# One pass of exponentials and gate for all tokens, and half of the columns turned by DMA

## The chip, the core and the metric

The kernel runs on one core of a Trainium2 chip. The core has a matrix engine (TensorE, PE in the profile; its weight loads are listed as PEld), a vector engine (VectorE, DVE), an engine for activation functions (ScalarE, ACT), a general one (GpSimd, POOL) and one that issues transfers (SyncE, SP). Each engine works through its own list of instructions in order, and engines wait for each other on semaphores. The transfers of all queues run on 16 DMA engines.

The metric is the time of the kernel on the device in microseconds (us); smaller is better. A changed kernel is compared with the kernel before on the same chip.

## The reference

All arithmetic is in float32. Eight sequences of 512 tokens with 512 features go through one block:

```python
xn = layernorm(x)                                   # x: (8, 512, 512)
# linear attention, 16 heads of 32
q, k, v = rotate(silu(xn @ Wq)), rotate(silu(xn @ Wk)), xn @ Wv
for chunk in chunks_of_128:                         # with per-head decay
    o = (q @ k.T * D) @ v + (q * decay_q) @ S
    S = lam_C * S + (k * decay_k).T @ v
s = group_rmsnorm(o * sigmoid(xn @ Wg1 @ Wg2)) * norm_weight @ Wo
# 16 experts, 4 of them per token, and a shared one
p = softmax(xn @ gate_w.T); w, e = top_k(p, 4); w = w / w.sum()
mixed = sum(w[r] * swiglu(xn, expert[e[r]]) for r in range(4))
shared = swiglu(xn, shared_expert) * sigmoid(xn @ shared_gate_w)
out = x + s * silu(mixed + shared)
```

Softmax over the 16 followed by the division through the sum of the four is the same as exponentials of the four logits less the largest one, divided by their sum. The kernel computes that.

## The kernel before, in words

A tile is 128 tokens; a sequence has four, and there are 32 in all. The work has these stages:

1. **To about 200 us: routing and shared expert of all eight sequences, beside the attention of sequence 0.** `norm` brings a sequence to mean 0 and variance 1 in place. `turn` transposes it on TensorE (four transposes of 128x128 per tile into one bank of PSUM, `psT`) and ScalarE copies the bank to `xT`, the transposed sequence. `route_1` multiplies it with the router weights (`plT`, 17 columns: 16 experts and the shared gate), `route_2` turns the result back (`pl`, copied to `lg`), `route_3` picks the four largest and makes their weights `w4` and one-hot masks. `share_1` and `share_2` compute the shared expert (`pg`, `pu`, `h`, `pys`), and its rows go to memory (`sh_d`). `halves` splits the upper 256 columns of each row into their 16-bit halves (`hs`) and writes them to `xn_d`, from where the expert blocks gather them.
2. **To about 240 us: `sort`** makes the places of all tokens in the lists of the experts, and sums the weights into rows that lie beside the tokens in `xn_d`.
3. **To about 310 us: attention of sequence 1**, with the tables of the lists made in between.
4. **To about 725 us: expert blocks** of 128 list entries: a gather, transposes (half by TensorE, half by a DMA on the 16-bit halves, joined by ScalarE in `join`), two matrix products and the weighted rows to `y_d`.
5. **To the end: attention of sequences 2 to 7**, beside `mixture`, which gathers four rows of `y_d` per token, adds them to the shared expert's row `m`, and applies Silu.

The order on TensorE in stage 1 is written out by hand: each group is issued `on_pe`, behind the last one. `first` is a generator of the pieces of routing and shared expert, and `along` takes the next one or two pieces between the pieces of the attention. On the other engines a scheduler orders the instructions at build time. It uses eight completion semaphores for the transfers of SyncE in turn, so that each transfer is issued only once the eighth before it is complete.

PSUM has eight banks: four of kind `a` and two of kind `d` that are taken in turn, one `m` and one `k`. A bank is free once its reader is done. ScalarE holds the table of one function at a time; the profile shows each change of it as ACT_TABLE_LOAD. Copies need none.

Lines that the prediction touches: 281 (transposes), 283 (copy of `psT`), 298 (`plT`), 314 (sigmoid of the gate), 331 (exponential), 357 and 637 (Silu of the shared expert, of keys and queries), 372 (shared rows times gate), 583 and 587 (values and their copy), 691 (scores `ps`), 738 and 742 (attention output `po` and its product with `on`), 706, 1076 and 1091 (the nearest rows for new operations), 1220 (mixture).

Of the kernel before, what the change touches and what calls it, by code (L numbers as in the profile page):

```python
# [10 lines left out]
F32 = mybir.dt.float32  # L11
# [3 lines left out]
U16 = mybir.dt.uint16  # L15
AF = mybir.ActivationFunctionType
ALU = mybir.AluOpType
AX = mybir.AxisListType

P = 128  # L20
B, N, D = 8, 512, 512
# [3 lines left out]
NC = N // C  # L25
NT = B * NC
KC = D // P
E, F, TOPK = 16, 128, 4
EA = E + 1
RK = HD  # L30
Q = 32
# [64 lines left out]
def tile_block(ctx: ExitStack, tc: tile.TileContext, a: dict, out: bass.AP):  # L96
    nc = tc.nc
# [3 lines left out]
    dram = ctx.enter_context(tc.tile_pool(name="dram", bufs=1, space=bass.MemoryType.DRAM))  # L101
# [3 lines left out]
    def bank(tag, name):  # L105
        return pp.tile([P, 512], F32, tag=tag, name=name, bufs={"a": 4, "k": 1, "m": 1, "d": 2}[tag])
# [6 lines left out]
    s_d = [dram.tile([N, D], F32, name=f"s_d{b}", tag=f"s_d{b}") for b in range(FIRST)]  # L113
    y_d = dram.tile([NB * P, D], F32, name="y_d", tag="y_d")
    at_d = dram.tile([P, TOPK * NT], I32, name="at_d", tag="at_d")

    def load(pool, name, shape, dt=F32):
        t = pool.tile(shape, dt, tag=name, name=name, bufs=1)
        flat = t if len(shape) == 2 else t.rearrange(
            "p a b -> p (a b)" if len(shape) == 3 else "p a b c -> p (a b c)")  # L120
        nc.sync.dma_start(flat, a[name])
        return t
# [17 lines left out]
    scr1 = left.enter_context(tc.tile_pool(name="scr1", bufs=1, side="left"))  # L140
    p1 = right.enter_context(tc.tile_pool(name="p1", bufs=1, side="right"))

    xs_of = {}

    def load_x(b):
        t = p1.tile([P, NC, D], F32, tag="x", name=f"x_{b}", bufs=3)
# [6 lines left out]
    ident = load(const, "ident", [P, P])  # L153
# [31 lines left out]
    wo = load_w(const, "wo")  # L185

    w4 = p1.tile([P, NT, TOPK], F32, tag="w4", name="w4")
    posi = p1.tile([P, TOPK, NT], I32, tag="posi", name="posi")

    sp = const.tile([P, 2, TOPK * NT], F16, tag="slot", name="sp")  # L190
# [27 lines left out]
        mybir.EngineType.Pool, mybir.EngineType.DVE, mybir.EngineType.Activation)  # L218


    xT_of, xT1_of, plT_of, lg_of, h1_of, sg_of = ({} for _ in range(6))
    oh = p1.tile([P, TOPK, E, NT], F32, tag="oh", name="oh")
    mask = p1.tile([P, E, NT], F32, tag="mask", name="mask")

# [33 lines left out]
    def halves(b):  # L258
        xs = xs_of[b]
        for t in range(NC):  # L260
            hs = p1.tile([P, D], U16, tag="hs", name=f"hs_{b}_{t}", bufs=4)
            with behind(POOL):
                nc.gpsimd.tensor_copy(
                    hs.rearrange("p (h d) -> p h d", h=2),
                    xs[:, t, D // 2 :].bitcast(U16).rearrange("p (d h) -> p h d", h=2))
            g = b * NC + t
            nc.sync.dma_start(xn_d[g * P : (g + 1) * P, D : 2 * D], hs)

    def turn(b):

        xs = xs_of[b]
        if b:
            xT = p1.tile([P, KC, N], F32, tag="xT1", name=f"xT1_{b}", bufs=2)
        else:
            xT = xT_of[b] = att.tile([P, KC, N], F32, tag="xT", name=f"xT_{b}", bufs=1)
        xT1_of[b] = xT
        for t in range(NC):
            ps = bank("a", f"psT_{b}_{t}")
            with on_pe():
                for k in range(KC):  # L280
                    nc.tensor.transpose(
                        ps[:, k * P : (k + 1) * P], xs[:, t, k * P : (k + 1) * P], ident)
            nc.scalar.copy(
                xT[:, :, t * P : (t + 1) * P], ps.rearrange("p (k n) -> p k n", n=P))
        if b:
            xs_of.pop(b)
            if b + 3 < B:
                load_x(b + 3)
            nc.sync.dma_start(xT_d[b], xT.rearrange("p k n -> p (k n)"))
# [16 lines left out]
    def route_2(b):  # L306
        lT = plT_of.pop(b)
        pl = bank("a", f"pl_{b}")
        with on_pe():
            nc.tensor.transpose(pl[:, :P], lT, ident)  # L310
        lg = p1.tile([P, NC, EA], F32, tag="lg", name=f"lg_{b}", bufs=2)
        nc.vector.tensor_copy(lg, pl[:, :P].rearrange("p (t q) -> p t q", q=Q)[:, :, :EA])
        sg = p1.tile([P, NC], F32, tag="sg", name=f"sg_{b}", bufs=2)
        nc.scalar.activation(sg, lg[:, :, E], AF.Sigmoid)
        sg_of[b] = sg
        lg_of[b] = lg

    def route_3(b):
        lg = lg_of.pop(b)
        mx = p1.tile([P, NC, 8], F32, tag="mx", name=f"mx_{b}", bufs=2)  # L320
        ix = p1.tile([P, NC, 8], U32, tag="ix", name=f"ix_{b}", bufs=2)
        for t in range(NC):
            nc.vector.max(mx[:, t, :], lg[:, t, :E])
            nc.vector.max_index(ix[:, t, :], mx[:, t, :], lg[:, t, :E])
        bt = slice(b * NC, (b + 1) * NC)
        nc.vector.tensor_copy(
            idx[:, :, bt].rearrange("p r t -> p t r"), ix[:, :, :TOPK])
        e4 = p1.tile([P, NC, TOPK], F32, tag="e4", name=f"e4_{b}", bufs=2)
        nc.vector.tensor_tensor(
            e4, mx[:, :, :TOPK], mx[:, :, 0:1].to_broadcast([P, NC, TOPK]), ALU.subtract)  # L330
        nc.scalar.activation(e4, e4, AF.Exp)
        den = p1.tile([P, NC], F32, tag="den", name=f"den_{b}", bufs=2)
        nc.vector.tensor_reduce(den, e4, axis=AX.X, op=ALU.add)
        nc.vector.reciprocal(den, den)
        nc.vector.tensor_tensor(
            w4[:, bt, :], e4, den.unsqueeze(2).to_broadcast([P, NC, TOPK]), ALU.mult)

        for q in range(TOPK):
            nc.vector.tensor_tensor(
                oh[:, q, :, bt], idx[:, q, bt].unsqueeze(1).to_broadcast([P, E, NC]),  # L340
                iota_e.unsqueeze(2).to_broadcast([P, E, NC]), ALU.is_equal)
        for q in range(1, TOPK):
            nc.vector.tensor_tensor(
                mask[:, :, bt], mask[:, :, bt] if q > 1 else oh[:, 0, :, bt], oh[:, q, :, bt],
                ALU.add)
# [14 lines left out]
        h1_of[b] = h  # L360

    def share_2(b):
        h, sg = h1_of.pop(b), sg_of.pop(b)
        xT1_of.pop(b)
        for t in range(NC):
            sh = p1.tile([P, D], F32, tag="sh1", name=f"sh1_{b}_{t}", bufs=6)
            py = bank("dama"[t], f"pys_{b}_{t}")
            with on_pe():
                nc.tensor.matmul(
                    py, lhsT=h[:, t * P : (t + 1) * P], rhs=sw[:, KC * 2 * F :],  # L370
                    start=True, stop=True)
            nc.scalar.activation(sh, py, AF.Copy, scale=sg[:, t : t + 1])
            nc.sync.dma_start(sh_d[b][t * P : (t + 1) * P, :], sh)


    def sort():

        wt = p1.tile([P, NT, E], F32, tag="h1", name="wt", bufs=2)
        wr = p1.tile([P, NT, E], F32, tag="sl", name="wr", bufs=2)
        for r in range(TOPK):  # L380
# [12 lines left out]
        for to, by, name in ((total, ones, "total"), (af, tri, "before")):  # L393
            ps = bank("a", f"p{name}")
# [572 lines left out]
    def first():  # L967
# [22 lines left out]
        next(sorting)  # L990

    sorting = sort()
    norm(0)
    turn(0)
    norm(1)
    halves(0)
    xs_of.pop(0)
    load_x(3)
# [174 lines left out]
    with tc.If(count > SURE):  # L1173
# [16 lines left out]
    comb = right.enter_context(  # L1190
        tc.tile_pool(name="comb", bufs=1, side="right", reuse_waits="tile"))

    place = comb.tile([P, TOPK, NT], I32, tag="place", name="place")
    nc.sync.dma_start(place.rearrange("p r t -> p (r t)"), at_d)

    def mixture(b, t):

        g = b * NC + t
        m = comb.tile([P, D], F32, tag="m", name=f"m_{b}_{t}", bufs=12)
        nc.sync.dma_start(m, sh_d[b][t * P : (t + 1) * P, :])  # L1200
        s = None
        if b < FIRST:
            s = comb.tile([P, D], F32, tag="s", name=f"s_{b}_{t}", bufs=4)
            nc.sync.dma_start(s, s_d[b][t * P : (t + 1) * P, :])
        ys = []
        for r in range(TOPK):
            yg = comb.tile([P, D], F32, tag="yg", name=f"yg_{b}_{t}_{r}", bufs=14)
            with behind(POOL):
                nc.gpsimd.indirect_dma_start(  # L1209
                    out=yg, out_offset=None, in_=y_d,  # L1210
                    in_offset=bass.IndirectOffsetOnAxis(ap=place[:, r, g : g + 1], axis=0))
            ys.append(yg)
            yield
        with behind(POOL):
            nc.gpsimd.tensor_tensor(ys[0], ys[0], ys[1], ALU.add)
        yield
        with behind(POOL):
            nc.gpsimd.tensor_tensor(ys[2], ys[2], ys[3], ALU.add)
        with behind(DVE):
            nc.vector.tensor_tensor(m, m, ys[0], ALU.add)  # L1220
        yield
        with behind(DVE):
            nc.vector.tensor_tensor(m, m, ys[2], ALU.add)
        yield
        with behind(ACT):
            nc.scalar.activation(m, m, AF.Silu)
        yield
        if s is not None:
            last(b, t, m, s)
        else:  # L1230
            m_of[b, t] = m
# [125 lines left out]
```

## Time and profile before

| | us |
|---|---|
| median of 3 runs | 1181.88 (1180.34 to 1182.98) |
| profiled execution, in all | 1189.85 |
| its span, first to last instruction | 1188.0 |
| TensorE busy in the span | 1146.2 |
| VectorE, ScalarE, GpSimd busy | 711.0, 490.4, 450.1 |
| TensorE busy in the first 297 us | 274.8 |

Profiling makes the execution some 8 us longer than the plain runs, so sums are made against the profiled span and carried over. "Busy" is the union of the times of an engine's instructions. In the lists of groups, a row has the line, engine and operation, the tiles written and read, the count, then busy time in us and the mean of one instruction in ns, and last the idle time before them with what ended it. In lists by time, the first number is the start, the second the duration, and square brackets give the idle time before and what ended it.

### The profile page before, as it was taken

The page shows a single profiled execution, that of the slowest core. Times are in us where ns is not written, and L with a number is a line of the kernel's source. Part 1 is how long each engine was busy: PE and PEld are TensorE (multiplying, and loading weights), DVE is VectorE, ACT ScalarE, POOL GpSimd, SP SyncE. Part 2 cuts the span into 40 slices and gives each one's busy share as a digit, 9 for nine tenths or more (in the row PEclk, how much of TensorE's full clock was granted, in tenths as well). Part 3 has the DMA queues.
Part 4 walks back from the last instruction along what each step waited for, and adds up shares of the span by engine and source line. Part 5 has one row for each costly group of instructions (what it writes and reads, how often), then busy time and mean ns, then how long its engine had stood idle before and what let it go on. Part 6 is the DMA issues. An engine that isn't in the chain of part 4 may idle for free. (4 is left out here: it accounts for less than half of the span.)

```text
span 1188.0 us, 21728 instructions
## 1 busy us (share of the span) xinstructions
PE 1146.2 (96%) x7780; PEld 698.9 (59%) x7780; DVE 711.0 (60%) x1517; ACT 490.4 (41%) x1069; POOL 450.1 (38%) x432
## 2 busy tenths in 40 slices
PE   7999899998999999999999999999999999999997
PEld 4445454455577777777777775555554545545553
DVE  6457553897234444444434444868879688597784
ACT  4445354263374444444434442352252432423541
POOL 3212003200223333333332331761886848858211
PEclk9999899999999999999999999999999999999999
DMA  9965241191659999998999986941846636535112
GB/s 345 339 221 182 102 145 69 30 372 64 207 149 229 227 226 219 227 231 225 216 228 224 223 224 191 322 137 46 283 126 180 213 96 237 168 111 149 31 36 72
DMA packets 163500, 217.42 MB, mean 183 GB/s; under 512 B 89537, under 2 KB 98881, under 8 KB 161473
## 3 DMA queue, kind: packets, MB, share of 16 engines
q1 hardware_dynamic: 141984, 144.10, 40.7%
q0 software_dynamic: 21120, 70.34, 21.8%
q10 hardware_dynamic: 288, 1.57, 0.4%
q8 instruction: 65, 1.06, 0.4%
q14 instruction: 43, 0.34, 0.1%
HBM read 125.71 MB, written 72.42 MB: 167 GB/s over the span
## 5 line engine op out<-in xcount | busy, mean ns | idle before, releaser
L1108 PE MATMUL pgu<-wexp,xt 128*128 x1088 | 258.5, 381 | 2.7 <-ACT xt L1089 2.0
L1108 PEld LDWEIGHTS pgu<-wexp,xt 128*128 128x128 f32 x1088 | 205.3, 190 | 92.4 <-issue 37.5
L1067 POOL DMA_INDIRECT xg<-xn_d,slot x79 | 75.1, 951 | 239.2 <-DVE y L1138 156.8
L1091 ACT COPY xt<-pl 128x512 uint16<-128x512 uint16 x136 | 104.3, 767 | 142.3 <-DMA pl<-xg 82.6
L1113 DVE TENSOR_TENSOR slb<-slb,pgu 128x128 f32<-128x128 f32 x136 | 39.1, 287 | 199.1 <-ACT slb L1112 154.6
L1209 POOL DMA_INDIRECT yg<-y_d,place x128 | 140.8, 1100 | 30.6 <-issue 19.4
L1129 PE MATMUL py<-wexp,hT 128*128 x272 | 139.2, 594 | 0.0
L583 PE MATMUL pv<-wv,xT 128*128 128x512 f32 x256 | 120.8, 608 | 5.3 <-DMA xT<-xT_d 3.0
L627 PE MATMUL pk<-xT,wk 128*128 128x512 f32 x256 | 118.3, 603 | 0.0
L627 PE MATMUL pq<-xT,wq 128*128 128x512 f32 x256 | 115.9, 593 | 0.3 <-PEq L1173 0.3
L781 PE MATMUL pw<-wo,on 128*128 128x512 f32 x224 | 100.5, 595 | 4.1 <-DVE m L1246 3.5
L1250 POOL TENSOR_TENSOR xo<-xo,m 128x512 f32<-128x512 f32 x31 | 45.1, 1454 | 142.3 <-DVE m L1246 135.0
L1067 POOL DMA_INDIRECT more<-xn_d,slot x57 | 54.0, 947 | 111.6 <-DVE y L1138 110.7
L716 DVE TENSOR_TENSOR sc<-ps,dmask 128x512 f32<-128x512 f32 x128 | 79.1, 677 | 2.7 <-PE ps L691 2.6
L627 PEld LDWEIGHTS pq<-xT,wq 128*128 128x128 f32 x256 | 47.2, 191 | 52.8 <-issue 51.6
L583 PEld LDWEIGHTS pv<-wv,xT 128*128 128x128 f32 x256 | 46.1, 192 | 51.8 <-issue 42.5
L1138 DVE TENSOR_SCALAR y<-py,xg 128x512 f32<-128x512 f32 x79 | 59.2, 750 | 28.3 <-PE py L1129 27.8
L627 PEld LDWEIGHTS pk<-xT,wk 128*128 128x128 f32 x256 | 46.2, 190 | 50.0 <-issue 47.6
L781 PEld LDWEIGHTS pw<-wo,on 128*128 128x128 f32 x224 | 41.3, 190 | 53.1 <-issue 45.4
L1112 ACT ACTIVATE slb<-pgu 128x128 f32<-128x128 f32 x136 | 37.9, 279 | 81.7 <-PE pgu L1108 81.0
L700 ACT COPY blocked<-state 32x96 f32<-32x96 f32 x96 | 30.7, 320 | 82.2 <-DVE state L695 77.1
L1138 DVE TENSOR_SCALAR y<-py,more 128x512 f32<-128x512 f32 x57 | 42.7, 749 | 17.7 <-PE py L1129 17.7
(172 smaller groups left out, 1783.0 us busy)
## 6 DMA issues: line engine op xcount, KB each, us to landing
y_d<-y SPq DMA_DIRECT2D x136, 256.0 KB
wexp<-in_experts SPq DMA_DIRECT2D x14, 768.0 KB
sh_d<-sh SPq DMA_DIRECT2D x32, 256.0 KB
m<-sh_d SPq DMA_DIRECT2D x32, 256.0 KB
xo<-in_x SPq DMA_DIRECT2D x32, 256.0 KB
out<-xo SPq DMA_DIRECT2D x31, 256.0 KB
x<-in_x SPq DMA_DIRECT2D x7, 1024.0 KB
xT_d<-xT SPq DMA_DIRECT2D x7, 1024.0 KB
```

The costliest lines, as they stand in the source:

```text
L583: nc.tensor.matmul(pv, lhsT=xT_of[b][:, k, t * P : (t + 1) * P], rhs=wv[:, k, :], start=(k == 0), stop=(k == KC - 1))
L627: nc.tensor.matmul(ps, lhsT=w[:, k, g * P : (g + 1) * P], rhs=xT_of[b][:, k, :], start=(k == 0), stop=(k == KC - 1))
L716: nc.vector.tensor_tensor(s, pss[j].rearrange("p (c t) -> p c t", t=C), dmask[:, g * HG + j].unsqueeze(1).to_broadcast([P, NC, C]), ALU.mult)
L781: nc.tensor.matmul(pw, lhsT=on_of[b][:, g, t * P : (t + 1) * P], rhs=wo[:, g, :], start=(g == 0), stop=(g == G - 1))
L1067: nc.gpsimd.indirect_dma_start(out=row(i), out_offset=None, in_=xn_d, in_offset=bass.IndirectOffsetOnAxis(ap=slot[:, i : i + 1], axis=0))
L1091: nc.scalar.copy(xt[:, KP:, :].bitcast(U16).rearrange("p k (t h) -> p h k t", h=2), turned(i).rearrange("p (h k) t -> p h k t", h=2))
L1108: nc.tensor.matmul(pg[:, : 2 * F], lhsT=xt[:, k, :], rhs=wflat[:, bass.ds(off + k * 2 * F, 2 * F)], start=(k == 0), stop=(k == KC - 1))
L1113: nc.vector.tensor_tensor(sl, sl, pg[:, F : 2 * F], ALU.mult)
L1129: nc.tensor.matmul(py, lhsT=hT_of.pop(i), rhs=wflat[:, bass.ds(off_of.pop(i) + KC * 2 * F, D)], start=True, stop=True)
L1138: gone.append(nc.vector.tensor_scalar(y, py, row(i).bitcast(F32)[:, bass.ds(at, 1)], None, ALU.mult).ins)
L1209: nc.gpsimd.indirect_dma_start(out=yg, out_offset=None, in_=y_d, in_offset=bass.IndirectOffsetOnAxis(ap=place[:, r, g : g + 1], axis=0))
L1250: nc.gpsimd.tensor_tensor(xo, xo, m, ALU.add)
```

## The change

- The exponentials, their sum, its reciprocal and the product no longer stand in `route_3` for each sequence: `route_3` only stores the logits less the largest, and `sort` does the rest once for all 32 tiles.
- The sigmoid of the shared gate is also taken once in `sort`. `share_2` stores the shared rows without the gate; the gate goes to memory (`sg_d`), is loaded for the last stage, and `mixture` multiplies there. The buffers of `sh1` fall from 6 to 4.
- From the third sequence on (`b > 1`), `turn` transposes only the lower 256 columns on TensorE, two tiles to a bank. The upper 256 are turned by a DMA from `hs`, tile by tile, and ScalarE joins the 16-bit halves into `xT`.

```diff
@@ halves
             g = b * NC + t
+            if b > 1:
+                turned_of[b, t] = p1.tile(
+                    [P, KC, P], U16, tag="turned", name=f"turned_{b}_{t}", bufs=4)
+                nc.sync.dma_start_transpose(turned_of[b, t], hs)
             nc.sync.dma_start(xn_d[g * P : (g + 1) * P, D : 2 * D], hs)
@@ turn
-        for t in range(NC):
-            ps = bank("a", f"psT_{b}_{t}")
+        turned = [turned_of.pop((b, t), None) for t in range(NC)]
+        ks = KC // 2 if turned[0] is not None else KC
+        for ts in ([range(t, t + KC // ks) for t in range(0, NC, KC // ks)]):
+            ps = bank("a", f"psT_{b}_{ts.start}").rearrange("p (t k n) -> p t k n", k=ks, n=P)
             with on_pe():
-                for k in range(KC):
-                    nc.tensor.transpose(
-                        ps[:, k * P : (k + 1) * P], xs[:, t, k * P : (k + 1) * P], ident)
+                for t in ts:
+                    for k in range(ks):
+                        nc.tensor.transpose(
+                            ps[:, t - ts.start, k], xs[:, t, k * P : (k + 1) * P], ident)
             nc.scalar.copy(
-                xT[:, :, t * P : (t + 1) * P], ps.rearrange("p (k n) -> p k n", n=P))
+                xT[:, :ks, ts.start * P : ts.stop * P].rearrange(
+                    "p k (t n) -> p t k n", n=P), ps)
+        for t in range(NC if ks < KC else 0):
+            nc.scalar.copy(
+                xT[:, ks:, t * P : (t + 1) * P].bitcast(U16).rearrange(
+                    "p k (n h) -> p h k n", h=2),
+                turned[t].rearrange("p (h k) n -> p h k n", h=2))
@@ route_2
-        sg = p1.tile([P, NC], F32, tag="sg", name=f"sg_{b}", bufs=2)
-        nc.scalar.activation(sg, lg[:, :, E], AF.Sigmoid)
-        sg_of[b] = sg
+        nc.scalar.copy(
+            sgs[:, b * NC : (b + 1) * NC],
+            pl[:, :P].rearrange("p (t q) -> p t q", q=Q)[:, :, E])
@@ route_3
-        e4 = p1.tile([P, NC, TOPK], F32, tag="e4", name=f"e4_{b}", bufs=2)
         nc.vector.tensor_tensor(
-            e4, mx[:, :, :TOPK], mx[:, :, 0:1].to_broadcast([P, NC, TOPK]), ALU.subtract)
-        nc.scalar.activation(e4, e4, AF.Exp)
-        den = p1.tile([P, NC], F32, tag="den", name=f"den_{b}", bufs=2)
-        nc.vector.tensor_reduce(den, e4, axis=AX.X, op=ALU.add)
-        nc.vector.reciprocal(den, den)
-        nc.vector.tensor_tensor(
-            w4[:, bt, :], e4, den.unsqueeze(2).to_broadcast([P, NC, TOPK]), ALU.mult)
+            w4[:, bt, :], mx[:, :, :TOPK], mx[:, :, 0:1].to_broadcast([P, NC, TOPK]),
+            ALU.subtract)
@@ share_2
-            sh = p1.tile([P, D], F32, tag="sh1", name=f"sh1_{b}_{t}", bufs=6)
+            sh = p1.tile([P, D], F32, tag="sh1", name=f"sh1_{b}_{t}", bufs=4)
...
-            nc.scalar.activation(sh, py, AF.Copy, scale=sg[:, t : t + 1])
+            nc.scalar.copy(sh, py)
@@ sort
+        nc.scalar.activation(w4, w4, AF.Exp)
+        den = p1.tile([P, NT], F32, tag="den", name="den")
+        nc.vector.tensor_reduce(den, w4, axis=AX.X, op=ALU.add)
+        nc.vector.reciprocal(den, den)
+        nc.vector.tensor_tensor(
+            w4, w4, den.unsqueeze(2).to_broadcast([P, NT, TOPK]), ALU.mult)
+        nc.scalar.activation(sgs, sgs, AF.Sigmoid)
+        nc.sync.dma_start(sg_d, sgs)
@@ mixture
+    sg = comb.tile([P, NT], F32, tag="sg", name="sg")
+    nc.sync.dma_start(sg, sg_d)
...
-            nc.vector.tensor_tensor(m, m, ys[0], ALU.add)
+            nc.vector.scalar_tensor_tensor(
+                m, m, sg[:, g : g + 1], ys[0], ALU.mult, ALU.add)
```

More of the change, by code (lines that the diff above doesn't have):

```diff
@@ L115, in tile_block @@
     at_d = dram.tile([P, TOPK * NT], I32, name="at_d", tag="at_d")
+    sg_d = dram.tile([P, NT], F32, name="sg_d", tag="sg_d")
     def load(pool, name, shape, dt=F32):
@@ L141, in tile_block @@
     p1 = right.enter_context(tc.tile_pool(name="p1", bufs=1, side="right"))
-    xs_of = {}
+    xs_of, turned_of = {}, {}
     def load_x(b):
@@ L187, in tile_block @@
     w4 = p1.tile([P, NT, TOPK], F32, tag="w4", name="w4")
+    sgs = p1.tile([P, NT], F32, tag="sgs", name="sgs")
     posi = p1.tile([P, TOPK, NT], I32, tag="posi", name="posi")
@@ L218, in tile_block @@
         mybir.EngineType.Pool, mybir.EngineType.DVE, mybir.EngineType.Activation)
-    xT_of, xT1_of, plT_of, lg_of, h1_of, sg_of = ({} for _ in range(6))
+    xT_of, xT1_of, plT_of, lg_of, h1_of = ({} for _ in range(5))
     oh = p1.tile([P, TOPK, E, NT], F32, tag="oh", name="oh")
@@ L362, in share_2 @@
     def share_2(b):
-        h, sg = h1_of.pop(b), sg_of.pop(b)
+        h = h1_of.pop(b)
         xT1_of.pop(b)
         for t in range(NC):
-            sh = p1.tile([P, D], F32, tag="sh1", name=f"sh1_{b}_{t}", bufs=6)
+            sh = p1.tile([P, D], F32, tag="sh1", name=f"sh1_{b}_{t}", bufs=4)
             py = bank("dama"[t], f"pys_{b}_{t}")
```

## The prediction

> **What bounds the kernel now.** I read the page first (shares by engine, slices), then the work by stage, then the gaps of TensorE, then the order in time around the gaps.
>
> ```profile
> PE 1146.2 (96%) x7780; PEld 698.9 (59%) x7780; DVE 711.0 (60%) x1517; ACT 490.4 (41%) x1069; POOL 450.1 (38%) x432
> ```
>
> TensorE is busy 96% of the span, so what it waits for, and what it is spared, sets the time. The change touches the stage up to 200 us (routing, shared expert, attention of sequence 0) and one VectorE instruction per tile after 770 us. Work by stage (time, busy us of PE, PEld, DVE, ACT, POOL, clock, DMA share, GB/s) around the two falls of the clock:
>
> ```profile
> 121.27:124.68 3.41, 0.15 (x8) 0.00 (x0) 3.27 (x25) 2.10 (x3) 0.00 (x0) 1.00 0.49 164
> 124.68:128.09 3.41, 2.78 (x4) 1.23 (x5) 3.08 (x6) 0.62 (x1) 0.00 (x0) 0.50 0.00 0
> ...
> 271.45:274.86 3.41, 0.46 (x1) 0.30 (x2) 3.41 (x9) 0.00 (x0) 0.00 (x0) 1.00 0.22 90
> 274.86:278.28 3.42, 3.42 (x10) 1.53 (x8) 2.06 (x4) 1.93 (x7) 0.00 (x0) 0.50 0.00 0
> ```
>
> A stretch of 3.41 us in which TensorE did at most 0.46 us of work is followed by one at clock 0.50; after the first, the next one too, up to 131.50. So a gap of 3 us or more is paid for twice. What makes the gap at 121 us, in order of time:
>
> ```profile
> 122.38 0.22 ACT L331 ACTIVATE e<-e 128x16 f32<-128x16 f32 x1 [2.16 <-DVE e L329]
> ...
> 123.91 0.60 ACT L637 ACTIVATE sq<-pq 128x512 f32<-128x512 f32 x1
> ...
> 125.31 6.76 PE L369 MATMUL pys<-sw,h 128*128 128x512 f32 x8 [3.89 <-DVE on L742]
> ```
>
> The exponential of four tiles waits for VectorE, the Silu behind it pays a table load (from 122.61), and VectorE's sum behind the exponential holds the product with `on`. TensorE, done with `po` at 121.42, stands still for 3.89 us, and then needs 6.76 us where the same eight instructions take 3.60 at full clock.
>
> **The change, part by part.** Savings first.
>
> (1) Transposes. 6 sequences lose 8 of 16 each.
>
> ```profile
> L281 PE MATMUL psT<-ident,x 128*128 128x128 f32 x128 | 18.2, 294 | 7.4 <-DMA ident<-in_ident 6.2 <-DVE sc L716 0.8 <-DVE x L234 0.4
> ...
> L331 ACT ACT_TABLE_LOAD x8 | 10.3, 1283 | 0.1
> ```
>
> In time, sixteen take 1.91 us, so eight are 0.95 us; times 6 is 5.7 us of TensorE, which has no slack here: minus 5.7.
>
> (2) ScalarE. In the changed kernel's instruction order the table loads before the end of the sorting fall from 27 to 6: 21 x 1.283 = 26.9 us less; twelve fewer copies of `psT` (598 ns each, 7.2). It gains 24 joins of 16-bit halves, which have a row (767 ns, in the block stage below): 18.4. Net minus 15.7 us on an engine that has slack, so only the gaps count. Here a rule and a row differ: the Trainium skill, "ScalarE: Activation LUTs", section What ACT_TABLE_LOAD costs, adds a drain of about 1380 ns to each load, which would make the relief 56 us. In this trace the Silu above starts 1.30 us after its load started, so I take 1.283. Either way it counts only where TensorE waits:
> - 26.9 us: `pv` waits 0.68 for `sh` behind a sigmoid's load. Gone: 0.68.
> - 101.6 us: `ps` waits 0.75 for `lT` behind scaled copies and a load. Gone: 0.75.
> - 195.0 us: `pv` waits 1.66 for `sh`. In the new order one sigmoid load still stands before `sh_7_2`: `lg` is ready at 193.06, copy 0.2, load 1.28, sigmoid 0.2, copy 0.6 give 195.6, a wait of 0.65. Gain 1.0.
>
> (3) The gap at 121 us. Count from the end H of `h` of sequence 4 (111.36 before). Now `pys` waits for the Silu `sq`, and in front of that on ScalarE stands the first join of sequence 6. Its rows are centred at the same distance from H as before, and SyncE issues `hs` at H+6.2 (117.54). What a transpose takes is shown by the block stage:
>
> ```profile
> 436.43 1.20 SPq L1076 DMA_TRANSPOSE pl<-more  x1
> ...
> 439.87 0.77 ACT L1091 COPY xt<-pl 128x512 uint16<-128x512 uint16 x1 [0.77 <-DMA pl<-more]
> ```
>
> From issue to its reader 3.4 us, at a DMA share of 0.9, and 1.20 us of SyncE against 0.4 for a plain `hs`. So: landed H+9.6, join 0.77, copy of `sgs` 0.2, Silu 0.6: `pys` starts at H+11.2. TensorE is done with `po` at H+9.1 (10.06 less the 0.95 of the removed transposes): wait 2.1. The other three transposes follow at SyncE, alternating with the writes of `hs` (1.6 us a pair), the last issued at H+11.5 and landed at H+14.7; behind it on ScalarE stand three `sh` copies and `lT`, whose banks `ps` needs: done at H+17.3, against TensorE's H+16.05, wait 1.2. Both are too short for a half clock. Before: 3.89 plus (131.50 - 125.31)/2 = 3.1. Gain 7.0 - 3.3 = 3.7.
>
> Sum of savings: 5.7 + 0.7 + 0.75 + 1.0 + 3.7 = 11.8.
>
> Now what it adds.
>
> (4) A new wait at sequence 2. Before:
>
> ```profile
> 55.37 3.60 PE L583 MATMUL pv<-wv,xT 128*128 128x512 f32 x8
> ...
> 58.90 1.08 PE L298 MATMUL plT<-xT,rt_w 128*32 128x128 f32 x32
> ...
> 59.01 0.59 ACT L587 COPY v<-pv 128x512 f32<-128x512 f32 x1 [1.74 <-PE pv L583]
> ```
>
> TensorE goes from `pv` straight to `plT`, as `xT` was complete. In the new order ScalarE has, behind the copy of that same `pv`, four `sh` copies (moved there, as `sh1` has 4 buffers, not 6) and then the four joins that `plT` needs for its second half. After `pv` ends: 0.1 + 0.51 (copy; four in a row take 2.05 in time) + 4 x 0.51 (`sh`) + 2.75 (joins; a successor starts 0.66 after one) = 5.4 us, then 0.35 of `plT`. Without a wait `plT` takes 1.08: stall 4.65. The transposes themselves are not last: SyncE issues the fourth at about 53.5 (each issue waits for the eighth before it; `sh_d` of tile 2 was done by 53.5), so it lands near 57, five us before its join. Plus 4.65.
>
> The Trainium skill, "TensorE: Matmul & The Clock Gate", section Part 1 (the HAM clock gate), speaks against the change here: one idle window of about 3.4 us halves the clock, and the window runs free. The rows above agree. A stall of 4.65 with a few small matmuls in it covers a window to 2.95 us or more in most phases, so I take one half-clock window, 1.7 us; bounds 0 and 3.4. By rule and rows alike this term is 1.7; without it the sum would be a clearer gain.
>
> (5) Later joins. Sequence 3: SyncE is held at `xT_d` of sequence 2 until the joins, then issues four `sh_d` and the transposes; the last lands near 74, needed at 81: free. Sequences 4 and 5: joins stand before `sk` and a Silu whose products end 2 to 3 us later: free. Sequence 7: the last transpose is issued behind the 1 MB load of `xT` and lands about 3 us after `pg`'s end; the Silu behind it is late, but `pu` runs 3.6 us more; 0.5 left.
>
> (6) VectorE, mixture: 32 sums become product and sum.
>
> ```profile
> L1220 DVE TENSOR_TENSOR m<-m,yg x32: 673/682/2358, 774.0 to 1124.9; 128x512 f32<-128x512 f32 x32
> ...
> L706 DVE SCALAR_TENSOR_TENSOR state<-state,lamc,pk x16: 211/246/248, 105.2 to 291.1; 128x32 f32<-128x32 f32 x16
> ```
>
> By the skill's "Vector Engine (DVE) Microarchitecture Reference", Points that are easy to get wrong, such an instruction with two fp32 sources in SBUF runs at half throughput: 0.53 us x 32 = 17 us more. The nearest row here takes one source from PSUM, so it cannot exclude that; 246 ns for 32 elements is some 0.07 above a plain form, so I take 0.07 x 32 = 2.2 us of VectorE, which is busy 78% there; TensorE waits for `m` twice only (3.5 us together): 0.3. Upper end 4.
>
> (7) The new chain in `sort` (Exp for all, sum, reciprocal, product) makes POOL's `wt` some 2.2 us later; POOL then idles 11.9 us for `at`, so nothing. The two small DMAs of the gate: nothing, SyncE has room.
>
> Sum: 11.8 - 4.65 - 1.7 - 0.5 - 0.3 = 4.6 us less. The profiled execution has a span of 1188.0 (1189.85 in all) and would go to 1183.4. It is 8 us above the median of the plain runs, 1181.88, and its half clock at 121 us need not be in all of them, so I carry over 4.4: **1177.5**.
>
> **Rivals.**
> - A, as above, 1177.5 (own range 1173.5 to 1180.5): 0.48.
> - B, slower: the transposes land late. Place: ScalarE's queue at sequence 6, where each us beyond 3.4 is paid twice (before `sq`, before the `sh` copies), and once more at sequences 5 and 7 after 1 to 2 us. It decides from about 2 us late (landing after 5.4 us). At 6.5 us: 2 x 3.1 + 2 + 1.7 for a half clock = 9.9, so 1187. For it: in the first 59 us the DMA share is 0.97 and 1.01, and the issue takes three times as long. Against: at 118 to 123 us the share is 0.2 to 0.9, no more than in the block stage. 0.22.
> - C, no change: the stall at 59 us opens two half-clock windows (1.7 more) and the 3.1 at 121 us is absent from most plain runs: 1182. 0.13.
> - D, larger gain: no half clock at 59 us (1.7) and transposes that land after 2.6 (1.6): 1174. 0.12.
> - E, the halved product and sum: at 875 to 925 us VectorE is busy 46.8 of 50; 2 to 4 us come through, 1180.5. 0.05.
>
> The change does what it says: the loads go, and half the columns leave TensorE from sequence 2 on; that is in the instruction order.
>
> **How the numbers follow.** About 0.2% (2.4 us) is what a measurement can tell from no change. Faster: 0.41 of A, D, 0.02 of E = 0.55. Same: 0.07 of A, 0.11 of C, 0.03 of E = 0.21. Slower: B and 0.02 of C = 0.24. Range 1171.5 to 1186: it takes in A, C, D, E and the lower half of B.
>
> **What would show it.** Right: `plT` of sequence 2 waiting 4 to 5 us for joins, with clock 0.5 after it; no 3.89 us gap behind `po` of group 0, but two of 1 to 2 us; psT at 80 instructions. Wrong: joins waiting on DMA for more than 3 us at sequences 4 to 6, or the product and sum above 1 us without POOL beside it.

## The result: 9.6 us slower, where 4.4 us faster was predicted

The changed kernel takes 1189.94 us (median of 11 runs, 1185.37 to 1196.98) against 1180.34 us for the kernel before on the same chip. The ratio is 1.0083, with a 95% interval of 1.0066 to 1.0099. Its profiled execution took 1192.82 us, 2.9 above its median, and has a span of 1191.0.

First the engine rows of its page: busy us, share of the span, instructions.

```profile
PE 1138.2 (96%) x7732; PEld 694.5 (58%) x7732; DVE 713.0 (60%) x1496; ACT 468.8 (39%) x1054; POOL 451.8 (38%) x432
```

ScalarE is busy 21.6 us less than before. TensorE is busy 8.0 us less than in the profile above (1146.2), but 2.5 us more than in a second, shorter profile of the kernel before (1135.7 of 1174.8; it is taken up below). Against both it stands idle longer, 52.8 us where they have 41.8 and 39.1, and its clock is halved in six windows of 3.41 us where each of them has three. The groups of the first 200 us show for what it waits (busy us, mean ns, then the idle time before and what ended it):

```profile
L296 ACT COPY xT<-turned 128x512 uint16<-128x512 uint16 x24 | 18.0, 772 | 32.2 <-DMA turned<-hs 32.2
L290 PE MATMUL psT<-ident,x 128*128 128x128 f32 x80 | 12.9, 315 | 11.1 <-DMA ident<-in_ident 6.8 <-DVE sc L733 4.1 <-DVE x L236 0.2
L290 PEld LDWEIGHTS psT<-ident,x 128*128 128x128 f32 x80 | 11.0, 164 | 15.1 <-DVE st L244 6.8 <-DVE sc L733 4.3 <-issue 3.2
L366 ACT ACT_TABLE_LOAD x2 | 2.6, 1283 | 0.0
```

The transposes fell from 128 to 80 and from 18.2 to 12.9 us, and the Silu of the shared expert loads its table twice instead of five times. The new row is the first. ScalarE's 24 joins take 18.0 us, and in front of 16 of them ScalarE stood idle for 32.2 us until a DMA transpose had landed. ScalarE works in order, so everything behind such a join waits as well. Three places show it. Sequence 5, in order of time:

```profile
109.33 0.77 ACT L296 COPY xT<-turned 128x512 uint16<-128x512 uint16 x1 [6.56 <-DMA turned<-hs]
...
112.48 0.76 ACT L296 COPY xT<-turned 128x512 uint16<-128x512 uint16 x1 [1.14 <-DMA turned<-hs]
113.12 0.58 ACT L366 ACTIVATE sl<-pg 128x512 f32<-128x512 f32 x1
113.75 3.70 PE L644 MATMUL pk<-xT,wk 128*128 128x512 f32 x8 [1.84 <-ACT sl L366]
```

The Silu of sequence 4 had its input `pg` at about 107.6 us. Three joins of sequence 5 stand ahead of it, the first of which waits 6.56 us for its transfer. `pk` takes the bank that this Silu reads, so TensorE stops for 1.84 us. At sequence 7 it is the same, but with more behind it:

```profile
149.81 1.20 SPq L272 DMA_TRANSPOSE turned<-hs  x1
...
152.20 2.72 SPq L382 DMA_DIRECT2D sh_d<-sh  x4
152.24 0.77 ACT L296 COPY xT<-turned 128x512 uint16<-128x512 uint16 x1 [2.26 <-DMA turned<-hs]
152.87 0.58 ACT L381 COPY sh<-pys 128x512 f32<-128x512 f32 x1
153.39 0.61 ACT L381 COPY sh<-pys 128x512 f32<-128x512 f32 x1
155.02 1.25 SPq L272 DMA_TRANSPOSE turned<-hs  x1
...
157.06 3.70 PE L362 MATMUL pg<-xT,sw 128*128 128x512 f32 x8
...
159.46 0.53 SPq L582 DMA_DIRECT2D xT<-xT_d  x1
...
160.56 1.80 SPq L272 DMA_TRANSPOSE turned<-hs  x1
...
166.49 0.76 ACT L296 COPY xT<-turned 128x512 uint16<-128x512 uint16 x1 [4.87 <-DMA turned<-hs]
167.12 0.58 ACT L366 ACTIVATE sl<-pg 128x512 f32<-128x512 f32 x1
167.73 0.69 DVE L368 TENSOR_TENSOR h<-sl,pu 128x512 f32<-128x512 f32 x1 [7.94 <-ACT sl L366]
...
169.00 2.48 DVE L733 TENSOR_TENSOR sc<-ps,dmask 128x512 f32<-128x512 f32 x4
169.74 1.97 PE L290 MATMUL psT<-ident,x 128*128 128x128 f32 x8 [4.12 <-DVE sc L733]
```

Read this from both sides. ScalarE's first join waits 2.26 us for SyncE's first transpose, and two copies of shared rows (`sh`) stand behind it. The writes of those rows (`sh_d`) stand in SyncE's list ahead of the second transpose, so SyncE waits for ScalarE in turn, but only for 1.0 us (0.7 and 0.3 in its list of waits). Most of the way to the second transpose at 155.02 is the issue of six other transfers. The last transpose follows at 160.56, behind a 1 MB load of `xT`, and lands 5.9 us later. The Silu, `h` and VectorE's `sc` are late in turn, and TensorE stops for 4.12 us. The third place is the one that the prediction knew: `plT` of sequence 2.

```profile
58.30 2.67 ACT L296 COPY xT<-turned 128x512 uint16<-128x512 uint16 x4
...
59.16 0.41 PE L313 MATMUL plT<-xT,rt_w 128*32 128x128 f32 x2 [2.71 <-ACT xT L296]
...
61.57 5.40 PE L362 MATMUL pg<-xT,sw 128*128 128x512 f32 x8
```

The clock halves behind this place, behind sequence 7, and at sequence 6, where `pys` waits 1.53 us and `ps` 1.89 and 0.49; not behind sequence 5. The stretches, with their length, busy us of PE, PEld, DVE, ACT and POOL, then the clock, the DMA share and GB/s:

```profile
58.23:61.64 3.41, 1.84 (x17) 0.84 (x17) 0.00 (x0) 2.73 (x5) 0.61 (x1) 1.00 0.83 269
61.64:65.06 3.42, 3.42 (x4) 1.40 (x5) 0.00 (x0) 1.55 (x2) 0.00 (x0) 0.50 1.05 419
129.91:133.32 3.41, 1.03 (x13) 0.79 (x16) 1.03 (x5) 2.35 (x5) 0.00 (x0) 1.00 0.53 197
133.32:136.74 3.42, 3.42 (x29) 2.16 (x23) 2.31 (x4) 0.00 (x0) 0.00 (x0) 0.50 0.39 151
164.04:167.46 3.42, 1.58 (x57) 1.27 (x56) 0.00 (x0) 0.97 (x2) 0.00 (x0) 1.00 0.68 165
167.46:174.28 6.82, 4.54 (x12) 2.99 (x13) 3.67 (x8) 1.41 (x3) 0.00 (x0) 0.50 0.18 77
```

The plain runs agree: the mean granted clock of a run was 0.990 at the median of the 11 of the changed kernel, and 0.993 in 35 runs of the kernel before, timed with the first experiments. By estimate that is 0.003 x 1185 = 3.6 us of the loss.

### The profile page after: what moved, and what is told of

It is laid out like the page before. It is cut to its first block, busy times and chain, and to the rows that moved or that the text cites. A ratio compares the mean times of both kernels' runs of the same rounds, so it can differ in the third digit from the quotient of the medians.

```text
span 1191.0 us, 21622 instructions
## 1 busy us (share of the span) xinstructions
PE 1138.2 (96%) x7732; PEld 694.5 (58%) x7732; DVE 713.0 (60%) x1496; ACT 468.8 (39%) x1054; POOL 451.8 (38%) x432
## 5 line engine op out<-in xcount | busy, mean ns | idle before, releaser
L1130 DVE TENSOR_TENSOR slb<-slb,pgu 128x128 f32<-128x128 f32 x136 | 39.1, 288 | 207.8 <-ACT slb L1129 207.7
L1155 DVE TENSOR_SCALAR y<-py,more 128x512 f32<-128x512 f32 x57 | 42.7, 749 | 18.2 <-PE py L1146 18.1
```

Of the source, the lines that this page charges most:

```text
L1130: nc.vector.tensor_tensor(sl, sl, pg[:, F : 2 * F], ALU.mult)
L1155: gone.append(nc.vector.tensor_scalar(y, py, row(i).bitcast(F32)[:, bass.ds(at, 1)], None, ALU.mult).ins)
```

## The experiments

All times below are medians. The ratio is to the kernel before on the same chip, with its 95% interval.

| kernel | us | ratio |
|---|---|---|
| changed kernel | 1189.94 | 1.0083 (1.0066 to 1.0099) |
| before, again | 1178.53 | 0.9995 (0.9982 to 1.0007) |
| exponentials and gate only | 1171.63 | 0.9937 (0.9916 to 0.9957) |
| exponentials only | 1172.53 | 0.9933 (0.9911 to 0.9954) |
| gate only | 1178.53 | 0.9978 (0.9959 to 0.9996) |
| turning only | 1188.26 | 1.0075 (1.0049 to 1.0100) |
| changed, turning in sequences 3 to 6 | 1176.84 | 0.9981 (0.9967 to 0.9995) |
| changed, turning in 3 and 4 | 1173.08 | 0.9933 (0.9906 to 0.9961) |
| changed, joins never wait | 1169.44 | 0.9928 (0.9900 to 0.9956) |
| changed, joins behind `psT` copies | 1174.21 | 0.9957 (0.9941 to 0.9974) |
| the same, turning from sequence 3 on | 1167.76 | 0.9912 (0.9883 to 0.9940) |
| before, turning from 3 on, joins behind | 1179.23 | 0.9987 (0.9968 to 1.0005) |

**Which part costs.** The kernel before was profiled a second time without any edit. The expectation was:

> The kernel before, profiled a second time. If the first profiled execution (1189.85 us, with half clocks at 121 and 274 us and the 3.89 us gap of TensorE at 121 us) was an unlucky one, as the eleven plain runs of before suggest (1178.5 to 1183.0), this profile shows a span near 1178 to 1182 us, and TensorE waits less than 3 us around 121 us with no half clock there: then most of the 4.7 us that the prediction booked as saved between 100 and 135 us was never there to save. If taking a profile itself costs this kernel 8 us, the span is near 1188 us again, with both half clocks.

It took 1176.89 us in the profiled execution, within its plain runs (1176.8 to 1182.07). So taking a profile need not add 8 us; the first profiled execution was a long one. But the other half of the expectation failed: the stall at 121 us is there again, at its full size, with both half clocks.

```profile
121.53 0.21 ACT L331 ACTIVATE e<-e 128x16 f32<-128x16 f32 x1 [2.15 <-DVE e L329]
...
124.46 6.67 PE L369 MATMUL pys<-sw,h 128*128 128x512 f32 x8 [3.88 <-DVE on L742]
```

It belongs to the kernel before, and is really there to save. The two halves of the change were then tried apart. Exponentials and gate without the turning (and with the six `sh1` buffers of the kernel before):

```diff
-            if b > 1:
+            if b >= B:
...
-            sh = p1.tile([P, D], F32, tag="sh1", name=f"sh1_{b}_{t}", bufs=4)
+            sh = p1.tile([P, D], F32, tag="sh1", name=f"sh1_{b}_{t}", bufs=6)
```

> The change without the DMA turning: exponentials and the gate's sigmoid once for all tokens, the gate multiplied in the mixture, sh1 with six buffers as before; all transposes on TensorE. Theory A (the turning is what costs): between -2 and +0.5 us against before, 1178.5 to 1181. Theory B (the mixture's scaled addition, with its late m and half clock at 983 us, carries a good part of the loss): +3 to +5 us, about 1184.

The ratio of 0.9937 is a gain of 7.4 us (0.0063 x 1180), more than theory A allowed. TensorE does not wait at the place any more; the Silu of the queries waits for nothing but its own product:

```profile
116.08 0.60 ACT L654 ACTIVATE sq<-pq 128x512 f32<-128x512 f32 x1 [0.84 <-PE pq L644]
116.70 1.08 PE L755 MATMUL po<-sc,v 128*32 128x128 f32 x32
117.71 3.70 PE L378 MATMUL pys<-sw,h 128*128 128x512 f32 x8
```

Theory B, the mixture, is out: this kernel has the same 32 scaled additions. The turning alone, as the diff of `halves` and `turn` with `sh1` at 4 buffers, in the kernel before:

> The kernel before with the DMA turning and ScalarE's joins alone; exponentials, sigmoid and gate stay per sequence, sh1 has four buffers. Theory A: +8 to +12 us, 1188 to 1192, with TensorE waiting at sequence 2 and at sequence 7 as in the changed kernel. Theory B: about +5 us, 1185.

1188.26, a ratio of 1.0075, as theory A had it. TensorE waits 2.50 us at `plT` of sequence 2, 2.46 at `pk`, 2.96 at `pys` and 2.25 at `po`, with half clocks at 60.5, 115.1, 128.8 and 159.5 us. Of these, `pys` waits at the place where the kernel before waits 3.88; the other three places are new. At sequence 7, which theory A named too, the wait is at `po`: the first join of that sequence waits 3.55 us ahead of two table loads and the copies of `sh`. `psT` waits only the 0.76 us that it waits in the kernel before. ScalarE stands in front of 9 joins here, for 17.1 us in all, at much the same price as the 32.2 us of the changed kernel: what counts is which work stands behind a wait. Two turned sequences less:

```diff
-            if b > 1:
+            if 2 < b < 7:
```

> The changed kernel, but sequences 2 and 7 are turned wholly on TensorE again; 3 to 6 keep the DMA turning. If the two long waits with their half clocks (2.71 + 0.63 us and then 1.7 at 56 to 65 us; 4.12 us and then 3.4 at 166 to 174 us, 12.5 in all) are what costs, and 16 more transposes cost 16 x 0.119 = 1.9 us, it takes 1189.9 - 12.5 + 1.9 = 1179, about as long as before. If the waits of sequences 4 to 6 (1.84, 1.53, 2.4 and a half clock of 1.7) or something outside the first 200 us carry the loss, it stays at 1185 or above.

1176.84, close to the 1179 of the first alternative: the two long waits are gone. But it is still 5.2 us above the kernel without any turning (ratios 0.9981 and 0.9937), and one wait is now longer:

```profile
106.86 0.78 ACT L296 COPY xT<-turned 128x512 uint16<-128x512 uint16 x1 [8.52 <-DMA turned<-hs]
...
110.55 0.58 ACT L366 ACTIVATE sl<-pg 128x512 f32<-128x512 f32 x1
111.18 2.08 PE L644 MATMUL pk<-xT,wk 128*128 128x512 f32 x2 [3.37 <-ACT sl L366]
```

**Which property of the joins.** First, the joins keep their work, but never wait for a transfer:

```diff
+    still = p1.tile([P, KC, P], U16, tag="still", name="still", bufs=1)
+    nc.vector.memset(still, 0)
...
-                turned[t].rearrange("p (h k) n -> p h k n", h=2))
+                still.rearrange("p (h k) n -> p h k n", h=2))
```

> The changed kernel with every DMA transpose still issued, but ScalarE's 24 joins read a constant tile, so that they never wait for a transpose (the upper half of each turned sequence is then not the tokens). If the price of the turning is ScalarE standing in front of a join until a transfer lands (16 waits of 32.2 us in all in the changed kernel's profile, the Silus and the gate copies behind them), most of the 18 us between the changed kernel and the one without turning goes: the waits of sequences 4 to 7 (1.84 + 1.53 + 2.4 + 4.12 us) and their half clocks (1.7 + 3.4), 15 us, leaving 1173 to 1177 us, with the wait at sequence 2 (2.7 us, joins behind four gate copies) still there. If it is the joins' own work (24 x 0.77 = 18.4 us of ScalarE) or the DMA traffic, it stays above 1184 us.

1169.44, below the range: 18 us less than the changed kernel (ratios 1.0083 and 0.9928). The joins take about the same time per instruction (791 ns against 772) and the transposes are all issued:

```profile
L298 ACT COPY xT<-still 128x512 uint16<-128x512 uint16 x24 | 17.3, 791 | 0.6 <-DMA xT_d<-xT 0.6
```

So ScalarE's work and the traffic can't carry the loss; most of it is the waiting. That they cost nothing is not shown: against the kernel without turning (0.9937) this one gains 1.1 us where the 48 spared transposes are worth 5.7, with intervals that overlap. This run does not isolate it from the place: with no transfer to count on, the scheduler also ordered the joins anew. Those of sequence 2 ran from 23 to 27 us, and so the wait at `plT` went too, against the expectation.

Next, the joins do wait for their data, but stand elsewhere in ScalarE's list:

```diff
-            nc.scalar.copy(
-                xT[:, ks:, t * P : (t + 1) * P].bitcast(U16).rearrange(
-                    "p k (n h) -> p h k n", h=2),
-                turned[t].rearrange("p (h k) n -> p h k n", h=2))
+            with behind(ACT):
+                nc.scalar.copy(
+                    xT[:, ks:, t * P : (t + 1) * P].bitcast(U16).rearrange(
+                        "p k (n h) -> p h k n", h=2),
+                    turned[t].rearrange("p (h k) n -> p h k n", h=2))
```

> The changed kernel with one constraint more: each join is issued behind the copy out of PSUM of the same sequence, so on ScalarE it stands after the Silu of the sequence before and after the two psT copies, instead of ahead of them. If the place in ScalarE's queue is the cause for sequences 4 to 7, their waits and half clocks (15 us) go and 1173 to 1178 us remain, with the wait at sequence 2 as it was; if the transfers themselves come too late for the reader, plT then waits for the joins instead and it stays above 1184 us.

1174.21. Nothing else was changed in the text, and 14.9 us are gone (ratios 1.0083 and 0.9957, times 1180). The traces place nearly all of it in the first stage: its last `pys` ends at 185.7 us instead of 199.5. Up to there TensorE and VectorE run the same lists as in the changed kernel; besides the joins, one copy of `sgs` has moved on ScalarE and a few transfers on SyncE, where the first transpose of sequence 7 now stands behind the writes of `sh`. At sequence 5 the transposes go out when they did before, counted from `pg`, but the Silu is now ahead of the joins, and no join waits any more:

```profile
106.65 0.60 ACT L367 ACTIVATE sl<-pg 128x512 f32<-128x512 f32 x1 [4.87 <-PE pg L363]
...
110.52 1.07 ACT L292 COPY xT<-psT 128x512 f32<-128x512 f32 x2 [3.27 <-PE psT L290]
110.75 3.60 PE L645 MATMUL pk<-xT,wk 128*128 128x512 f32 x8
110.96 1.20 SPq L272 DMA_TRANSPOSE turned<-hs  x1
111.48 2.69 ACT L297 COPY xT<-turned 128x512 uint16<-128x512 uint16 x4
```

The group of all joins of this kernel, against 32.2 us of waiting in the changed one:

```profile
L297 ACT COPY xT<-turned 128x512 uint16<-128x512 uint16 x24 | 16.4, 778 | 0.0
```

The transposes don't go out earlier for it. At sequence 7:

```profile
148.66 3.70 PE L363 MATMUL pg<-xT,sw 128*128 128x512 f32 x8
...
152.63 1.89 SPq L272 DMA_TRANSPOSE turned<-hs  x1
...
159.76 2.63 ACT L297 COPY xT<-turned 128x512 uint16<-128x512 uint16 x4
```

Counted from the start of `pg`, the last transpose is issued after 3.97 us here, and after 3.50 in the changed kernel (157.06 and 160.56). So the gain comes from the place of the joins and not from earlier transfers. `plT` of sequence 2 still waits 2.71 us, as expected. Without that sequence, that is with `if b > 2:` on top:

> As the kernel before it in this list, and sequence 2 is turned on TensorE, so that the turning starts with the fourth sequence. If both causes are right, the 5 us at sequence 2 go as well: 1176 - 5.0 + 0.95 = about 1171 us, and with nothing left over the 40 transposes that TensorE still saves would show against the kernel without turning (1171.6 - 40 x 0.119 = 1166.8 us). If half clocks or later waits take it back, 1174 us or more.

1167.76, 5.3 us less than the one before (0.9957 and 0.9912), and the fastest complete kernel here: 0.9912 of the kernel before, 0.0088 x 1180 = 10.4 us. `plT` of sequence 2 follows `pv` with no wait and no half clock there. That it beats the kernel without turning (0.9937) by the 4.8 us of 40 transposes is not shown: the difference is 3.0 us and the intervals overlap.

And with `if 2 < b < 5:` in the changed kernel, its joins where they were:

> The changed kernel with only sequences 3 and 4 turned by DMA, the two in which no TensorE wait was seen. If a turned sequence without a wait gains its 8 transposes, 2 x 8 x 0.119 = 1.9 us against the kernel without turning: 1171.6 - 1.9 = 1169.7 us. If the turning costs even there (order on ScalarE and SP, half clocks), 1172 us or more.

1173.08 decides nothing. Its interval (0.9906 to 0.9961) covers both 1169.7 and 1172.

**What the gain consists of.** Exponentials once, with sigmoid, gate and transposes as before:

> The kernel before with only the exponentials taken once in the sort; the sigmoid and the scaling by the gate stay per sequence, no turning. If the stall of 3.88 us at 121 us and the half clock behind it (3.0) come from the exponential that stands in ScalarE's list between the keys and the queries and waits for VectorE, this part alone brings most of the 8.2 us that exponentials and gate bring together: 1172 to 1174 us. If the table loads and scaled copies of the gate are what counts, about 1178 us.

1172.53: the whole gain of the two edits together (0.9933 alone, 0.9937 with the gate). TensorE's stall of 3.88 us has shrunk to 0.23:

```profile
119.77 0.60 ACT L637 ACTIVATE sq<-pq 128x512 f32<-128x512 f32 x1
120.42 3.70 PE L363 MATMUL pys<-sw,h 128*128 128x512 f32 x8 [0.23 <-ACT sq L637]
```

The gate alone, with exponentials per sequence:

> The other part alone: sigmoid once in the sort and the gate multiplied in the mixture, the exponentials per sequence as before, no turning. If the exponential is the cause of the stall at 121 us, the stall stays and only the small waits go (0.68 + 0.75 + part of 1.66): 1177 to 1179 us. If the gate counts, 1173 us.

1178.53, a gain of 2.6 us (0.0022 x 1180). The stall stays, as the exponential still stands ahead of the Silu and waits for VectorE:

```profile
119.37 0.21 ACT L346 ACTIVATE e<-e 128x16 f32<-128x16 f32 x1 [2.20 <-DVE e L344]
...
122.30 5.40 PE L384 MATMUL pys<-sw,h 128*128 128x512 f32 x8 [3.88 <-DVE on L759]
```

Last, the turning with well placed joins in the kernel before, without the other two edits:

> The kernel before with the DMA turning from the fourth sequence on and each join behind its psT copies, but exponentials, sigmoid and gate per sequence. If the place of the joins was all that was wrong with the turning, it gains its 40 x 0.119 = 4.8 us here too: 1175 us. If the joins also need the room that the table loads leave on ScalarE, waits come back and it stays at 1179 us or above.

1179.23, with an interval that includes no change. The joins wait for no transfer here either. The gain of 4.8 us is outside the interval, so the second alternative is nearer. In the profile `pys` waits 3.93 us at 120 us, as in the kernel before, and small waits for ScalarE appear at `pys` of sequence 2 (0.61, for `sk`) and at `po` (1.25, for `sh`). These two take back 1.9 of the 4.8 us; what takes the rest is not shown.

## Why the prediction was wrong

The sum that the runs give, with ratios times 1180: exponentials and gate -7.4; the place of the joins at sequences 4 to 7 +14.9; sequence 2 +5.3; what is left of the turning -3.0. These are four steps from the changed kernel back to the one before, so that they must add up to its own ratio, +9.8; the sum is no check.

The traces give one, up to the last `pys` of the first stage, against the second profile of before. New are 19.2 us: the waits and half clocks of term 4 (3.34 + 1.7), of sequence 6 (1.53 + 2.38 + 1.7), and of term 5 (1.84 + 3.35 + 3.4). Gone are 13.7: transposes 5.3, the stall at 121 us with its half clock 7.0, small waits 1.4. That leaves +5.5, and the last `pys` ends at 199.5 instead of 194.0. So some 4 of the 9.6 us lie behind that stage.

- **Term 5 is the step that failed.** It held the later joins for free at sequences 3, 4 and 5, and worth 0.5 at 7. It looked at when each join's own product is due, and let the Silu behind it be late as long as another product ran. Measured: 1.84 us at sequence 5; at sequence 7 4.12 instead of the 0.77 that `psT` waited before, and two windows of half clock, 3.4 us: 8.6 in all. At sequence 7 the last transpose was counted to land some 3 us after the end of `pg`; it landed 5.7 us after, as it was under way for 5.9 us and not for some 3.4. Sequences 3 and 4 cost no TensorE wait, as said.
- **Term 3** had the gap right and its successors wrong in one thing. Waits of 2.1 and 1.2 were predicted, and 1.53 and 2.38 (1.89 + 0.49) were measured. "Both are too short for a half clock" was false: the clock halved at 133.32. The gain of 3.7 became 7.0 - 3.9 - 1.7 = 1.4. Without the joins the place gives back all of its 7 us, so the turning took away most of what the exponential brought.
- **Term 4**, the wait at sequence 2, was right in place, cause and clock, and a little too large: 4.65 + 1.7 = 6.35 predicted; 3.34 (2.71 + 3 x 0.21) and 1.7 for the half clock in the trace; by removal 5.3, or 6.2 with the 0.95 of the transposes that the removal gives up.
- **Term 1** was right in size as work: 5.3 of 5.7 us left TensorE. **Term 2** was 2.4; the gate alone brought 2.6, and the waits of 0.68 and 0.75 are gone in it. On top of the exponentials it adds nothing that can be seen.
- **Term 6** was right: the scaled addition takes 744 ns at the median against 682, so 0.06 more, where 0.07 was taken. The halved rate that the Trainium skill ("Vector Engine (DVE) Microarchitecture Reference", Points that are easy to get wrong) would have meant is not seen here. The waits of `pw` for `m` were 6.2 us in the profile of after, but 5.4 in the second one of before.
- **The base.** "Profiling makes the execution some 8 us longer" was wrong, but harmless: up to 200 us the two profiles of before agree within 1.0 us, and the terms lie there.

Rival B had the mechanism and the sign: ScalarE's queue at sequences 5, 6 and 7, at 1187. It got 0.22, because it was thought to need transfers of more than 5.4 us, and the DMA share spoke against that. The share was right: the median from issue to landing was 3.0 us in the changed kernel, as far as its trace places the landings. Most of the transfers were not slow; the joins stood too early. One was slow, the last of sequence 7 with 5.9 us, and the longest stall stands behind it; but with the joins moved it is issued no earlier, and nothing waits for it. The sign "joins waiting on DMA for more than 3 us at sequences 4 to 6", named as what would make the prediction wrong, came true at 5 (6.56) and 6 (3.96).

What stays open: what the loss behind the first stage consists of. In the changed kernel's profile some of it lies behind 310 us. The blocks' `pgu` waits 8.9 us for `xt` there, against 0.4 to 5.4 in the other profiles, twice for about 3 us. With one profile of it, that may be this execution alone; it was not tried.

## What to carry to other kernels

An instruction that joins what a transfer brings belongs, in an in-order engine's list, behind everything that is ready before the transfer lands; ask of every new wait what stands behind it, not only when its own result is due. Here moving the joins was enough; the transfers did not have to come sooner. And a removed stall is only gained where nothing else of the change stands in the same place.

## What the runs showed of the hardware that was not expected

The clock does not need an idle window to fall. Laid on the grid of its changes (3.41 us), the 13 profiles hold, between 16 and 1150 us, 29 windows at full clock with less than 1.5 us of TensorE work, and 28 of them were followed by a half clock; of 38 with 1.5 to 2.0 us it was 3, and of some 4200 with more it was 11. So about 1.9 us of standing still in one window, in one or several pieces, was enough in nearly every case. The few busier ones need not hold a long gap at all; in the kernel that turns sequences 3 to 6, waits of 0.67 and 0.49 us among small products were in such a one:

```profile
126.66:130.07 3.41, 2.25 (x62) 1.79 (x61) 1.79 (x10) 2.88 (x7) 0.00 (x0) 1.00 0.55 173
130.07:133.48 3.41, 3.41 (x30) 2.67 (x31) 1.59 (x3) 0.07 (x1) 0.00 (x0) 0.50 0.56 212
```
